# Half of an attention's transposes moved from TensorE to VectorE's 32x32 blocks and a trip to DRAM

## The chip, the cores and the metric

One core of a Trainium2 chip runs the whole kernel. The metric is the device time of one execution in microseconds; the median of three runs before the change is 898.99 us (898.84 to 899.18).

## The reference, cut to what matters

The kernel is one decoder layer on 16 sequences of 256 tokens, width 256, in float32: a self-attention on fixed keys and values with squared ReLU, a cross-attention, and a feed-forward layer with routed low-rank adapters, each followed by a layer norm. The change is in the cross-attention, which has 16 heads of 16 channels:

```python
logits = einsum('bhqd,bhkd->bhqk', Q, K) * scale
D = clip(frac[:, None, :] - frac[:, :, None], -0.2, 0.2)
attn = gamma * logits + delta * (ap * max(D, 0) + an * min(D, 0))
probs = softmax(attn, axis=-1)
out = einsum('bhqk,bhkd->bhqd', probs, V)
```

`ap` and `an` are one number for each head. The logits come with queries on the partitions, so that the maximum over keys is a reduction along a row. The product with V needs the probabilities the other way round, with keys on the partitions. So each 256x256 block of each head has to be transposed.

## The kernel before, in words

The program's order on each engine is the order in which the code issues instructions (a manual schedule). Each engine takes its own instructions in that order and waits at the first whose inputs or buffers are not ready. SyncE (SP) issues nearly all DMAs and is such a queue too.

The first 252 us are the self-attention. Then come 64 *groups*, four for each sequence (a *batch* `b`; `og = n % 4` counts its groups). A group is four heads. One turn of the loop over `n`, here called a round, works on several groups at once: `now` (group n), `nxt` (n+1), `last` (n-1) and `older` (n-2).

- `logits` (L650): 16 small matmuls (two records each in the profile) of `now` into four PSUM banks, one for each head. They add to what `positive` (L640, ScalarE) has put there, the positive part of the bias.
- `negative` (L628 on GpSimd, L633 on ScalarE): the negative part of the bias of `nxt`, into the tile `neg`.
- `maxima` (L667, VectorE): eight instructions that add the bank and `neg`, write the sum over `neg` (also called `t`) and keep the row maximum `mx`. When the two of a head are done, `nxt.positive` may overwrite that head's bank.
- `subtract` (L682): row maximum off, two heads on GpSimd, two on VectorE.
- `turned` and `exps` (L692, L699): four 128x128 transposes on TensorE (PE) for a head into a PSUM tile `ps_b`, then the exponential on ScalarE on the way into the tile `pT`. A group has 16 such transposes.
- `attend` (L708): eight matmuls with the values and a column block of ones, which gives the softmax's denominator. After a batch's second and fourth group `keep` copies the accumulators (L721), and after the fourth `gather` sends them through DMAs: `sums`, and eight `v`.

The ScalarE order in a round was written by hand as a string: `s0` is `nxt.positive(0)`, `e0` is `last.turned(0)` and `last.exps(0)`, `g` a copy of the router's logits in some rounds:

```python
for act in ("e0 s0 s1 e1 s2 s3" if eager else "s0 s1 g e0 e1 s2" if ff and part == 0
            else "s0 s1 g e0 s2 e1 s3").split():
```

Heads 2 and 3 of `last` follow at the end of the round. In between, the round works on pieces of other batches: queries, keys, values and the output projection, each a PE step of four matmuls with a copy behind it. Their DMAs stand on SP in this order over a batch: og 1 `sums` and eight `v`; og 2 `rows`, eight `kM` (keys of the next batch, laid out for the row groups) and eight `invs` (the denominators' inverses, spread over partitions from DRAM); og 3 `cT` and the fractions or clipped biases of a later batch.

From n = 15 on, feed-forward work is woven in: eight rounds (`part` 0 to 7) for 512 tokens. Parts 2 and 3 (`halved`) hold the two large pieces of the inner layer, in the same four banks between `maxima` and `positive`; parts 4 to 7 hold the outer layer (`finish`). In parts 5 and 7 (`apart`) `attend` is left to the next round, which then has two. Rounds 0 to 14 are called plain rounds.

The accumulating tiles `ps_b` turn in two or three buffers, `neg` in three, `pT` in two.

Of the kernel before, what the change touches and what calls it, by code (L numbers as in the profile page):

```python
# [9 lines left out]
FP = mybir.dt.float32  # L10
AF = mybir.ActivationFunctionType
ALU = mybir.AluOpType
AX = mybir.AxisListType

P = 128
# [3 lines left out]
BIG = 3.0e38  # L19
# [3 lines left out]
def tile_decoder_layer(ctx: ExitStack, tc: tile.TileContext, a: dict, out: bass.AP):  # L23


    nc = tc.nc
    NTOK, C = a["x"].shape
    B, S = a["frac"].shape
# [29 lines left out]
    def tile_v(tag="V"):  # L58
        return psV.tile([P, 512], FP, tag=tag, name="ps_v")
# [155 lines left out]
    drams = ctx.enter_context(tc.tile_pool(name="drams", bufs=2, space=bass.MemoryType.DRAM))  # L215
# [16 lines left out]
    if True:  # L232
# [16 lines left out]
        class Block:  # L249
            def __init__(self, tb):  # L250
                self.tb = tb
# [169 lines left out]
    if True:  # L421
# [8 lines left out]
        class Batch:  # L430
# [183 lines left out]
        class Group:  # L614
            def __init__(self, batch, og):
                self.batch = batch
                self.o, self.i = divmod(og, 2)

            def head(self, g):
                return 8 * self.o + 2 * g + self.i  # L620
# [40 lines left out]
            def maxima(self):  # L661

                self.t = self.neg
                self.mx = small.tile([P, 4, 2], FP, tag="mx", name="mx")
                for g in range(4):
                    for j in range(2):
                        nc.vector.tensor_tensor_reduce(  # L667
                            out=self.t[:, g, j, :],
                            in0=banks[g][:, j * S : (j + 1) * S],
                            in1=self.neg[:, g, j, :],  # L670
                            scale=1.0,
                            scalar=-BIG,
                            op0=ALU.add,
                            op1=ALU.max,
                            accum_out=self.mx[:, g, j : j + 1],
                        )

            def subtract(self, halves):
                for g, eng in zip((0, 2), halves):
                    rows = self.t[:, g : g + 2].rearrange("p g j k -> p (g j) k")  # L680
                    top = self.mx[:, g : g + 2].rearrange("p g j -> p (g j)").unsqueeze(2)
                    eng.tensor_tensor(rows, rows, top.to_broadcast([P, 4, S]), ALU.subtract)  # L682
# [18 lines left out]
            def attend(self):  # L701

                batch = self.batch
                if self.i == 0:
                    batch.av = tile_v()
                for k in range(2):
                    for g in range(4):
                        nc.tensor.matmul(  # L708
                            batch.av[32 * g : 32 * g + 32, self.i * S : (self.i + 1) * S],
                            lhsT=batch.va[:, k, self.head(g), :],  # L710
                            rhs=self.pT[:, g, k * S : (k + 1) * S],
                            start=(k == 0),
                            stop=(k == 1),
                        )
# [7 lines left out]
                    if self.o == 1:  # L722
                        batch.gather()

        MADE = 5
# [229 lines left out]
    with tc.manual_schedule():  # L955
# [5 lines left out]
        for j in range(WARM):  # L961
# [17 lines left out]
        for tb in range(NB):  # L979
            now = rows_in[tb]  # L980
# [6 lines left out]
            if tb > 1:  # L987
                last = rows_in[tb - 2]
# [14 lines left out]
            if tb + 1 < NB:  # L1003
                nxt = rows_in[tb + 1]
# [33 lines left out]
            for m in range(8):  # L1038
                c, n2 = divmod(m, 4)
# [22 lines left out]
        pm = ctx.enter_context(tc.tile_pool(name="pm", bufs=2))  # L1062
# [4 lines left out]
        FUSED, FIRST = NB - 2, 15  # L1067
# [6 lines left out]
        for n in range(N + 2):  # L1074
            now, nxt, last, older = (
                groups[n + d] if 0 <= n + d < N else None for d in (0, 1, -1, -2)
            )
            large_piece, small_piece, more = pieces(n)
            tb, part = divmod(n - FIRST, 8)
            ff = rows_out[tb] if 0 <= tb < FUSED or (tb == FUSED and part < 2) else None  # L1080
            halved = ff and part in (2, 3)
# [7 lines left out]
            b, og = divmod(n, 4)  # L1089
# [34 lines left out]
            if n == 29:  # L1124
                by[NB] = scaling_of(rest_mv, newton(rest_mv, near_rest, 8), 8)
            if halved:
                for g in range(2):
                    last.turned(g)
                    last.exps(g)
                if part == 2:  # L1130
                    ff.route()
                now.subtract((nc.gpsimd, nc.vector))
                if part == 2:
                    ff.biased()
                if done:
                    done.ready(newton(done.mv, done.near, 4))
                ff.inner(part - 2, range(0, 3))
                if part == 2:
                    ff.turn_um()
                ff.inner(part - 2, range(3, 4))  # L1140
                ff.lora(part - 2, scalar=(0,))
                for g in range(4):
                    nxt.positive(g)
                older.attend()
            else:


                eager = n in (12, 13, 14)
                for act in ("e0 s0 s1 e1 s2 s3" if eager else "s0 s1 g e0 e1 s2" if ff and part == 0
                            else "s0 s1 g e0 s2 e1 s3").split():  # L1150
                    g = int(act[1:] or 0)
                    if act == "g":
                        if ff and part == 1 and n < N:
                            ff.keep_gates()
                    elif act[0] == "s":
                        if act == "s3" and n == N:
                            older.attend()
                        if nxt:
                            nxt.positive(g)
                    elif last:  # L1160
                        last.turned(g)
                        last.exps(g)
                if prep and prep.tb:
                    prep.rows()
# [27 lines left out]
                prep.rows()  # L1192
            if done and not halved:
                done.ready(newton(done.mv, done.near, 4))
            if ff and part >= 4:
# [139 lines left out]
```

## Time and profile before

| | us |
|---|---|
| median of three runs | 898.99 |
| profiled execution, its own time | 898.66 |
| its span, first to last instruction | 896.9 |
| self-attention, up to the first logits | 252.4 |
| plain rounds of groups 2 to 14 (263.2 to 342.4) | 79.2 |
| rounds of groups 15 to 62, with feed-forward work (342.4 to 813.0) | 470.6 |
| the rest (813.0 to 896.9) | 83.9 |

| engine | busy us | share of the span |
|---|---|---|
| PE matmuls | 885.6 | 99% |
| VectorE (DVE) | 713.0 | 79% |
| ScalarE (ACT) | 567.1 | 63% |
| GpSimd (POOL) | 398.8 | 44% |

The profile holds one execution. A group of instructions is shown as line, engine, operation, output and inputs, count, then busy us and mean ns of one, then the engine's idle time ahead of them and what ended it. A line of the timeline starts with the start and the duration in us. DMAs took 15% of the 16 DMA engines' time, 41 GB/s in the mean.

### The profile page before, as it was taken

Reading aid. Unit: us, or ns where it says so; the run is one execution under the profiler, and the core shown is the slowest. Engines: PE = TensorE matmul, PEld = TensorE weight load, DVE = VectorE, ACT = ScalarE, POOL = GpSimd, SP = SyncE. Lnnn points to the kernel's source line nnn. Section 1 sums busy time; section 2 is a strip of 40 time slices with the busy share of each in tenths; the row PEclk is TensorE's granted clock in tenths of the full one; section 3 lists DMA queues with packets and bytes.
Section 4 is the critical chain, followed back from the end, with each engine's and each line's share of the span. In section 5 each row is a group of like instructions: output and inputs, shape, how many; then the busy total and the mean of one; then the engine's idle time right before and its main releaser. Section 6 shows DMA issues by size and latency. Waiting matters only on the chain.

```text
span 896.9 us, 21381 instructions
## 1 busy us (share of the span) xinstructions
PE 885.6 (99%) x8092; PEld 550.0 (61%) x8092; DVE 713.0 (79%) x1986; ACT 567.1 (63%) x951; POOL 398.8 (44%) x385
## 2 busy tenths in 40 slices
PE   8999999999999999999999999999999999999997
PEld 4334444444466777577668757766875776586555
DVE  6879889988779899788777877877798787778344
ACT  5766777777787888376556836666684665566111
POOL 1101223422489899435534644563465456344010
PEclk9999999999999999999999999999999999999999
DMA  5501110110001222011111202011110201111001
GB/s 138 156 1 42 53 43 25 30 49 1 14 1 55 71 69 57 14 42 25 33 50 39 48 14 67 21 36 46 43 48 14 67 20 38 44 29 43 23 2 46
DMA packets 44200, 37.15 MB, mean 41 GB/s; under 512 B 14913, under 2 KB 40001, under 8 KB 44097
## 3 DMA queue, kind: packets, MB, share of 16 engines
q1 hardware_dynamic: 43520, 35.52, 14.5%
q8 instruction: 64, 1.05, 0.5%
q10 hardware_dynamic: 576, 0.26, 0.1%
q14 instruction: 40, 0.32, 0.1%
HBM read 21.07 MB, written 6.03 MB: 30 GB/s over the span
## 4 chain that ended last, share of the span: by engine, by line
PE 97%; ACT 2%; DVE 1%; issue 0%; POOL 0%; DVEq 0%; ACTq 0%; POOLq 0%
PE ps_b L692 13%; PE ps_a L339 13%; PE ps_v L358 12%; PE ps_l L887 12%; PE ps_l L650 8%; PE ps_b L920 7%; PE ps_v L708 7%; PE ps_v L920 5%; PE ps_b L601 3%; PE ps_b L497 3%; PE ps_b L471 3%; PE ps_b L519 3%; PE ps_l L900 2%; PE ps_b L814 1%; PE ps_b L458 1%; PE ps_b L799 1%
## 5 line engine op out<-in xcount | busy, mean ns | idle before, releaser
L628 POOL TENSOR_SCALAR neg<-dneg,aneg,delta 128x512 f32<-128x512 f32 x217 | 182.0, 852 | 181.7 <-PE ps_b L692 127.3
L667 DVE CUSTOM_DVE_ANT_0 neg<-ps_l,neg 128x256 f32<-128x256 f32 x512 | 181.5, 420 | 27.7 <-PE ps_l L650 24.6
L640 ACT ACTIVATE ps_l<-dpos,apos_d 128x512 f32<-128x512 f32 x256 | 172.8, 687 | 42.0 <-DVE mx L667 26.9
L699 ACT ACTIVATE pT<-ps_b 128x512 f32<-128x512 f32 x256 | 142.3, 591 | 57.4 <-PE ps_b L692 56.2
L348 DVE TENSOR_TENSOR pr<-pr 128x1024 f32<-128x1024 f32 x128 | 153.8, 1243 | 30.2 <-ACT pr L347 29.8
L347 ACT ACTIVATE pr<-ps_a 128x1024 f32<-128x1024 f32 x128 | 125.0, 1026 | 52.9 <-PE ps_a L339 52.5
L692 PE MATMUL ps_b<-ident,neg 128*128 128x128 f32 x1024 | 139.0, 277 | 2.3 <-ACT pT L699 2.3
L692 PEld LDWEIGHTS ps_b<-ident,neg 128*128 128x128 f32 x1024 | 113.6, 141 | 37.9 <-POOL neg L628 12.7
L682 POOL TENSOR_TENSOR neg<-neg,mx 128x1024 f32<-128x1024 f32 x65 | 125.3, 1929 | 18.1 <-DVE mx L667 16.9
L339 PE MATMUL ps_a<-xnT,kT 64*64 64x512 f32 x1024 | 124.6, 593 | 1.0 <-ACT xnT L324 0.4
L358 PE MATMUL ps_v<-pr,vv 64*64 64x512 f32 x1024 | 122.7, 589 | 0.0
L887 PE MATMUL ps_l<-xt,wi 128*128 128x512 f32 x248 | 111.7, 596 | 0.0
L682 DVE TENSOR_TENSOR neg<-neg,mx 128x1024 f32<-128x1024 f32 x63 | 99.0, 1572 | 0.6
L413 POOL TENSOR_TENSOR hid<-hid,bo 128x256 f32<-128x256 f32 x32 | 43.7, 1368 | 105.0 <-ACT hid L245 86.4
L358 PEld LDWEIGHTS ps_v<-pr,vv 64*64 64x64 f32 x1024 | 45.1, 133 | 64.4 <-issue 54.5
L339 PEld LDWEIGHTS ps_a<-xnT,kT 64*64 64x64 f32 x1024 | 42.0, 133 | 65.2 <-issue 52.4
L887 PEld LDWEIGHTS ps_l<-xt,wi 128*128 128x128 f32 x248 | 45.3, 190 | 49.4 <-issue 44.4
L650 PE MATMUL ps_l<-kM,qT 32*64 32x256 f32 x2048 | 74.2, 387 | 0.0
L373 POOL TENSOR_TENSOR xt<-xt,half 128x512 f32<-128x512 f32 x15 | 19.1, 1274 | 119.2 <-ACT half L372 119.2
L920 PE MATMUL ps_b<-wof,hT 128*128 128x256 f32 x304 | 68.4, 380 | 0.0
L708 PE MATMUL ps_v<-pT,vaug 128*32 128x256 f32 x1024 | 66.5, 384 | 0.0
L913 DVE TENSOR_SCALAR hT<-ps_l,wib 128x512 f32<-128x512 f32 x43 | 29.8, 745 | 44.0 <-PE ps_l L900 44.0
(131 smaller groups left out, 1075.2 us busy)
## 6 DMA issues: line engine op xcount, KB each, us to landing
cT<-in_ctxT SPq DMA_DIRECT2D x16, 256.0 KB
kM<-keys SPq DMA_DIRECT2D x128, 32.0 KB
v<-raw SPq DMA_DIRECT2D x128, 32.0 KB
invs<-rows SPq DMA_DIRECT2D x128, 32.0 KB
x<-in_x SPq DMA_DIRECT2D x7, 512.0 KB
out<-x SPq DMA_DIRECT2D x7, 512.0 KB
frow<-in_frac SPq DMA_DIRECT2D x16, 128.0 KB
wi<-in_wiT SPq DMA_DIRECT2D x1, 1024.0 KB
```

The costliest lines, as they stand in the source:

```text
L339: nc.tensor.matmul(sc[64 * k : 64 * k + 64, h, :], lhsT=kT[64 * h : 64 * h + 64, q, hf * P + 64 * k : hf * P + 64 * k + 64], rhs=self.xnT[ ...
L348: nc.vector.tensor_tensor(pr, pr, pr, ALU.mult)
L358: nc.tensor.matmul(self.acc[k][64 * h : 64 * h + 64, :], lhsT=vv[64 * k : 64 * k + 64, hf, 64 * q : 64 * q + 64], rhs=pr[64 * k : 64 * k + ...
L628: nc.gpsimd.tensor_scalar(self.neg[:, g], self.batch.dneg, aneg[:, h : h + 1], delta, ALU.mult, ALU.mult,)
L640: nc.scalar.activation(banks[g], self.batch.dpos.rearrange("p j k -> p (j k)"), AF.Copy, scale=apos_d[:, h : h + 1],)
L650: nc.tensor.matmul(banks[g][64 * h : 64 * h + 64, j * S : (j + 1) * S], lhsT=self.batch.qT[rows, self.o, j * P + 64 * h : j * P + 64 * h + ...
L667: nc.vector.tensor_tensor_reduce(out=self.t[:, g, j, :], in0=banks[g][:, j * S : (j + 1) * S], in1=self.neg[:, g, j, :], scale=1.0, scalar ...
L682: eng.tensor_tensor(rows, rows, top.to_broadcast([P, 4, S]), ALU.subtract)
L692: nc.tensor.transpose(ps[:, k * S + j * P : k * S + (j + 1) * P], self.t[:, g, j, k * P : (k + 1) * P], ident,)
L699: nc.scalar.activation(self.pT[:, g, :], self.ps[g], AF.Exp)
L887: nc.tensor.matmul(self.banks[g], lhsT=wi[:, c, f * P : (f + 1) * P], rhs=self.xT[:, c, :], start=(c == 0), stop=False,)
L920: nc.tensor.matmul(ps[:, 0:C], lhsT=self.hT[f][:, j * P : (j + 1) * P], rhs=wof[:, f, :], start=(f == 0), stop=(f == FC - 1),)
```

## The change

From group 2 on (`DIRECT = 2`, `self.direct`), heads 0 and 1 of a group go another way:

- `maxima` of these two heads writes the negated sums and keeps their minimum.
- `exp_rows` (new, four ScalarE instructions) takes the exponential in place, in rows, with the minimum as the bias and the scale -1. So there is no `subtract` on VectorE; the one for heads 2 and 3 is on GpSimd.
- `blocks` (new): one VectorE transpose of 128x1024 in blocks of 32x32, into the tile `z` (one buffer), and one DMA of 512 KB from `z` to DRAM.
- `fetch` (new): in the next round four DMAs of 128 KB, each to 32 partitions of `pT`, bring the blocks to their places. They read what the DMA of `blocks` wrote.
- `attend` reads these two heads out of `pT` in runs of 32 elements.
- Heads 2 and 3 keep their PE transposes and `exps`, which now come in the middle of the ACT string, and there are four `exp_rows` (`x0 x1`) between them and `s2`. GpSimd makes all four of `negative`.

SP's order over a batch of plain rounds is now: fetch, write (og 0); fetch, `sums`, `v`, write (og 1); fetch, `rows`, `kM`, `invs`, write (og 2); fetch, write, `cT` and others (og 3).

```diff
+                self.direct = 4 * batch.b + og >= DIRECT
...
+                    minus = self.direct and g < 2
...
-                            scale=1.0,
-                            scalar=-BIG,
+                            scale=-1.0 if minus else 1.0,
+                            scalar=BIG if minus else -BIG,
                             op0=ALU.add,
-                            op1=ALU.max,
+                            op1=ALU.min if minus else ALU.max,
...
+            def exp_rows(self, g):
+                for j in range(2):
+                    nc.scalar.activation(
+                        self.t[:, g, j, :], self.t[:, g, j, :], AF.Exp,
+                        bias=self.mx[:, g, j : j + 1], scale=-1.0,
+                    )
+
+            def blocks(self):
+                self.z = pm.tile([P, 4, 2, 4, 32], FP, tag="z", bufs=1, name="z")
+                nc.vector.transpose(
+                    self.z.rearrange("p n c h q -> p h c n q"),
+                    self.t[:, 0:2].rearrange("p g j (c n k) -> p (g j) c n k", c=2, k=32),
+                )
+                self.away = drams.tile([P, 4, 4 * P // 2], FP, tag="blocks", name="away_z")
+                nc.sync.dma_start(
+                    out=self.away, in_=self.z.rearrange("p n c h q -> p n (c h q)")
+                )
+
+            def fetch(self):
+                self.pT = pm.tile([P, 4, 2 * S], FP, tag="pT", name="pT")
+                self.ps = {}
+                self.pD = self.pT[:, 0:2].rearrange("p g (a c h q) -> p (g a) c h q", a=2, c=2, q=64)
+                for n in range(4):
+                    nc.sync.dma_start(
+                        out=self.pT[32 * n : 32 * n + 32, 0:2].rearrange("k g (a e) -> k (g a) e", a=2),
+                        in_=self.away[:, n].rearrange("(r k) e -> k r e", k=32),
+                    )
+
             def subtract(self, halves):
-                for g, eng in zip((0, 2), halves):
+                for g, eng in ((2, nc.gpsimd),) if self.direct else zip((0, 2), halves):
...
+                        rhs = self.pT[:, g, k * S : (k + 1) * S]
+                        to = batch.av[32 * g : 32 * g + 32, self.i * S : (self.i + 1) * S]
+                        if self.direct and g < 2:
+                            rhs = self.pD[:, :, k, g, :].rearrange("p r (j q) -> p j r q", j=2)
+                            to = to.rearrange("p (j r q) -> p j r q", j=2, q=32)
...
+            if last and last.direct:
+                last.fetch()
...
-                nxt.negative(4 if 1 <= n < FIRST - 1 or (ff and part < 2) else 3)
+                nxt.negative(4 if nxt.direct or 1 <= n < FIRST - 1 else 3)
...
-                for act in ("e0 s0 s1 e1 s2 s3" if eager else "s0 s1 g e0 e1 s2" if ff and part == 0
-                            else "s0 s1 g e0 s2 e1 s3").split():
+                if n >= N or not now.direct:
+                    acts = "e0 s0 s1 e1 s2 s3" if eager else "s0 s1 g e0 s2 e1 s3"
+                    if ff and part == 0:
+                        acts = "s0 s1 g e0 e1 s2"
+                else:
+                    acts = "s0 e0 s1 g e1 x0 x1 s2" + ("" if ff and part == 0 else " s3")
...
+            if now and now.direct and not halved:
+                now.blocks()
             if ff and part >= 4:
                 ff.finish(part - 4, tile_v() if apart else None)
-            if last:
+            if last and not last.direct:
                 for g in range(2, 4):
                     last.turned(g)
                     last.exps(g)
```

In the halved rounds `exp_rows` and `blocks` stand beside `subtract`, ahead of the inner layer's pieces.

More of the change, by code (lines that the diff above doesn't have):

```diff
@@ L707, in attend @@
                     for g in range(4):
+                        rhs = self.pT[:, g, k * S : (k + 1) * S]
[3 more added lines that the diff above has]
+                            to = to.rearrange("p (j r q) -> p j r q", j=2, q=32)
                         nc.tensor.matmul(
-                            batch.av[32 * g : 32 * g + 32, self.i * S : (self.i + 1) * S],
+                            to,
                             lhsT=batch.va[:, k, self.head(g), :],
-                            rhs=self.pT[:, g, k * S : (k + 1) * S],
+                            rhs=rhs,
                             start=(k == 0),
@@ L723, in keep @@
                         batch.gather()
-        MADE = 5
+        MADE, DIRECT = 5, 2
         batches = [Batch(b) for b in range(B)]
@@ L1126, in tile_decoder_layer @@
             if halved:
-                for g in range(2):
+                for g in range(2, 4) if last.direct else range(2):
                     last.turned(g)
@@ L1131, in tile_decoder_layer @@
                     ff.route()
+                if now.direct:
+                    for g in range(2):
+                        now.exp_rows(g)
                 now.subtract((nc.gpsimd, nc.vector))
+                if now.direct:
+                    now.blocks()
                 if part == 2:
@@ L1148, in tile_decoder_layer @@
                 eager = n in (12, 13, 14)
-                for act in ("e0 s0 s1 e1 s2 s3" if eager else "s0 s1 g e0 e1 s2" if ff and part == 0
-                            else "s0 s1 g e0 s2 e1 s3").split():
+                if n >= N or not now.direct:
[4 more added lines that the diff above has]
+                    acts = "s0 e0 s1 g e1 x0 x1 s2" + ("" if ff and part == 0 else " s3")
+                for act in acts.split():
                     g = int(act[1:] or 0)
@@ L1159, in tile_decoder_layer @@
                             nxt.positive(g)
+                    elif act[0] == "x":
+                        if now:
+                            now.exp_rows(g)
                     elif last:
+                        if last.direct:
+                            g += 2
                         last.turned(g)
@@ L1194, in tile_decoder_layer @@
                 done.ready(newton(done.mv, done.near, 4))
+            if now and now.direct and not halved:
+                now.blocks()
             if ff and part >= 4:
                 ff.finish(part - 4, tile_v() if apart else None)
-            if last:
+            if last and not last.direct:
                 for g in range(2, 4):
```

## The prediction

> **What bounds the kernel now.** I read the page first: busy shares, the chain that ended last, the costliest groups.
>
> ```profile
> span 896.9 us, 21381 instructions
> PE 885.6 (99%) x8092; PEld 550.0 (61%) x8092; DVE 713.0 (79%) x1986; ACT 567.1 (63%) x951; POOL 398.8 (44%) x385
> PE 97%; ACT 2%; DVE 1%; issue 0%; POOL 0%; DVEq 0%; ACTq 0%; POOLq 0%
> L692 PE MATMUL ps_b<-ident,neg 128*128 128x128 f32 x1024 | 139.0, 277 | 2.3 <-ACT pT L699 2.3
> ```
>
> TensorE is never idle and carries the chain; the transposes that the change halves are in it. Next I asked for the chain in one round of the attention without feed-forward work (a round: from one group's logits to the next one's), and for each engine's busy time in such a round and in the eight rounds of a feed-forward cycle.
>
> ```profile
> 306.19 1.05 PE ps_l L650 x32
> 307.24 1.00 PE ps_v L708 x16
> 308.24 1.02 PE ps_b L692 x8
> 309.26 1.73 PE ps_b L601 x8
> 310.99 1.03 PE ps_b L692 x8
> ```
>
> ```profile
> 306.10:311.95 5.85, 5.85 (x73) 4.19 (x72) 5.39 (x21) 5.51 (x11) 5.43 (x5) 1.00 0.16 57
> ```
>
> ```profile
> sum 79.10, PE 79.10 PEld 55.43 DVE 64.53 ACT 49.50 POOL 39.22; mean PE 9.89 PEld 6.93 DVE 8.07 ACT 6.19 POOL 4.90
> ```
>
> (The columns behind the stretch are busy us of PE, PEld, DVE, ACT and POOL.) A plain round takes 5.83 us, with DVE, ACT and POOL close behind at 5.4 to 5.5. A feed-forward cycle has room. Last, the timelines of ACT in a plain round and of SP (which issues the DMAs) in one batch of four groups:
>
> ```profile
> 302.49 1.38 ACT L640 ACTIVATE ps_l<-dpos,apos_d 128x512 f32<-128x512 f32 x2 [1.22 <-DVE mx L667]
> 303.81 0.58 ACT L699 ACTIVATE pT<-ps_b 128x512 f32<-128x512 f32 x1
> 305.38 0.69 ACT L640 ACTIVATE ps_l<-dpos,apos_d 128x512 f32<-128x512 f32 x1
> 305.99 1.08 ACT L699 ACTIVATE pT<-ps_b 128x512 f32<-128x512 f32 x2
> ```
>
> ```profile
> 286.44 0.69 SPq L561 DMA_DIRECT2D sums<-raw  x1
> 287.18 5.86 SPq L569 DMA_DIRECT2D v<-raw  x8
> 293.15 0.52 SPq L579 DMA_DIRECT2D rows<-inv  x1
> 293.78 5.62 SPq L513 DMA_DIRECT2D kM<-keys  x8
> 299.45 3.84 SPq L587 DMA_DIRECT2D invs<-rows  x8
> ```
>
> SP holds each small DMA for about half a microsecond, so a batch costs it some 17 us; today nobody waits for that.
>
> **Removed from PE.** Eight transposes a group: 1.02 us, for 62 groups 63 us, all on today's chain.
>
> **Removed and added beside it.** VectorE loses one subtract (1.57 us mean) and gains one transpose of 128x1024; no row shows one. The subtract of that size took 1.22 us alone and 2.06 us at its slowest (304.47); I take 1.3, near the undisturbed row, so VectorE gets no fuller. It waits there for the `exp_rows` (6.04 us after the round's start, below); behind it stand the next round's maxima, due at 8.65, so up to 2.6 us are free. GpSimd gets a fourth `negative` (0.85 us) in the feed-forward rounds, where it has 4.9 of 9.9 us busy: nothing, and ACT loses a 0.72 us instruction there. Minima in place of maxima are as many instructions: nothing. `attend` reads two heads in runs of 32 elements; between 0 and 0.5 us (half of its 1.00 us doubled), taken as 0. The 1 MB a group is some 3 us of DMA at 347 GB/s (below): it fits a round.
>
> **ACT's circuit.** Before, a round's last two `exps` came after the fourth `positive`. Now everything comes before it: s0 e0 s1 e1, four `exp_rows`, s2, s3 (s is `positive`, e is `exps`), and the next logits need s3. The first s starts 2.20 us after the logits start (300.29 to 302.49). A `positive` is 0.62 (four took 2.53), the last 0.69, an `exps` 0.50. An `exp_rows` (128x256, SBUF to SBUF, bias from a tile) lies between the gT copy of 128x256, 0.27 to its successor, and L245 (x from hid) with bias and scale from tiles, 12.5 us for 24 = 0.52; I take 0.40, the middle, since it has one of the two. Sum: 2.20 + 0.62 + 0.50 + 0.62 + 0.50 + 1.60 + 0.62 + 0.69 = **7.35 us**. PE would need 5.83 - 1.02 = 4.81. So a plain round gets longer by this alone (6.83 with 0.27, 7.83 with 0.52).
>
> **SP's queue.** Each group adds a write w (512 KB, SBUF to DRAM), and a fetch f of four DMAs that cannot be issued before w has landed; SP stands at that wait, and all behind it in the queue (`sums`, `v`, `rows`, `kM`, `invs`, the next w) stands too. The order in the plain rounds, by group of the batch: f, w | f, sums, v, w | f, rows, kM, invs, w | f, w. For w I take the 512 KB store issued at 616.51: transfers stop by 619.2, so 2.65 us.
>
> ```profile
> 617.50:618.30 0.80, 0.80 (x10) 0.23 (x16) 0.00 (x0) 0.00 (x0) 0.00 (x0) 1.00 0.97 347
> 618.30:619.20 0.90, 0.90 (x22) 0.17 (x10) 0.08 (x1) 0.12 (x1) 0.00 (x0) 1.00 0.74 259
> 619.20:620.00 0.80, 0.80 (x17) 0.30 (x9) 0.80 (x2) 0.77 (x2) 0.00 (x0) 1.00 0.00 0
> ```
>
> f: four issues at 0.46 (invs: 3.84 for eight) = 1.85; landed 3.6 after the first, as the 512 KB load issued at 129.93, whose traffic ends by 133.6. Bounds: 0.40 an issue (`cT`) to 0.75 (`v` at 6.08 for eight).
>
> The circuit of a plain batch, from the end of its first group's transpose: w 2.65, f 1.85, wait for the `raw` copy 0.4, sums and v 6.45 (5.8 to 6.75 in the trace), w 2.65, f 1.85, rows, kM and invs 9.8 (0.34 to 0.52, 5.6, 3.84), w of the third group 2.65, its f landing 3.6; then `attend` 1.00, one head's transposes and their release 0.7 (ACT's e0 waits for them, and all of ACT behind it), e0 s1 e1 1.62, `exp_rows` 1.6, VectorE's transpose 1.3: 38.1, about **38 us a batch**, against 24.5 now (275.81 to 300.29). Seen from the rounds: four of 7.35, plus 1.85 of wait at the fourth group, plus 6.9 in the next batch's first round, where PE stands at `attend` of the third group.
>
> From group 2 to 15 are 13 rounds, now 79.2 us (263.2 to 342.4): 13 x 7.35 + 2 x (1.85 + 6.9) = 113.1, **+34 us**.
>
> **A feed-forward cycle.** Its rounds now last 7.98, 6.73, 14.49, 14.05, 9.57, 8.13, 9.99, 8.13 us. Each becomes the longer of itself less 1.02 and the ACT circuit. The first, with two `attend`s before e0 and two copies before s3, makes 9.4; the second has the gT copy, 7.7; the two long ones 13.47 and 13.03; then 8.55, 7.35, 8.97, 7.35. In the long rounds SP's waits are covered by feed-forward matmuls. In the eighth they are not: f until 6.95, rows to invs until 16.7, so w of that group starts at 16.7 instead of 7.4, lands at 19.35, f at 22.95 after the round's start; PE is at that `attend` at 7.35 + 9.4 + 1.05 = 17.8. **5.15 us of stall** make the second round 12.9. Sum 81.0 against 79.07: +1.9. For the first cycle (78.8 now) +2.2, for four +7.3, for the last (75.2 now, few pieces left) +5.4: **+15 us**. The rounds after group 63 are a chain of feed-forward matmuls (78.5 of 83.9 us busy): 0.
>
> **Clock.** PE now gets gaps. Granted clock is 1.00 all along, and in the tail it is 1.00 from 891.5 to 893.5, with no matmul in it, and 0.51 after. Eight stalls above 5 us could each make the following `attend` and transpose (1.5 us) twice as long: 0 to 12 us, and up to 29 more if the 2.5 us gaps of the plain rounds count too (13 x 2.2: 9.6 in place of 7.35). I take 6.
>
> [...]
>
> **The sum.** The profiled execution took 898.66 us, 0.33 below the median 898.99. 898.66 + 34 + 15 + 6 = 953.7; I say **953 us**.
>
> **Rivals.**
> *PE stays the bound.* DMAs and ACT hide; 898.7 - 63 = **835 us**. For it: a 99% busy PE and two rounds of grace between a group's exp and its `attend`. Against it: 7.35 us of ACT in front of logits that PE could start after 4.81. It needs the instructions before s3 to be near 2.5 us shorter, and SP never late.
> *ACT's circuit binds, SP does not.* If w and f always land in time, the stalls go: plain 13 x 7.35 - 79.2 = +16, cycles 81.0 - 5.15 = 75.8, six of them 455 in place of 471, -16: **about 899 us**, no change; with `exp_rows` at 0.27 about 880. This is the other side's likeliest form; it decides where a plain batch costs SP less than the four rounds' 29.4 us, not the 34 that 4 x (2.65 + 1.85) + 6.45 + 9.8 make.
> *Dearer all round.* Clock halved in the plain rounds and issues at 0.6: **about 1000 us**.
>
> **How the numbers follow.** Forecast 0.73 (own range 920 to 985), dearer 0.07, ACT's circuit alone 0.12 (a third of it within 0.2%), PE bound or near it 0.08. 0.2% is about what a measurement of this kernel can tell from no change. Faster 0.16, same 0.04, slower 0.80. The range from 897 to 1000 leaves out the faster 0.16 and 0.04 above.
>
> **What would show it.** After the change: PE well under 90% busy from 263 on; ACT, SP's waits or DMA landings in the chain; PE waiting for a DMA ahead of `attend` (pT from the blocks tile), 5 to 7 us once a batch; plain rounds of 7 us or more; SP in the timeline standing between w and f; granted clock under 1.00 somewhere. I am wrong if plain rounds stay under 6 us, if `attend` never waits, or if the transpose takes over 3 us (then VectorE is the bound).

## The result, and the profile after

The changed kernel takes **1050.24 us** (median of 4 runs, 1046.81 to 1052.71) against 899.09 for the kernel before (898.84 to 899.58): 1.168 times as long, 95% interval 1.1644 to 1.1711. The prediction said 953 us and a range up to 1000. The sign was right, the size was not: +151 us in place of +54.

From the page of the changed kernel's profiled execution (span; busy time by engine; granted clock in 40 slices; the chain that ended last; three groups):

```profile
span 1048.4 us, 21128 instructions
...
PE 917.2 (87%) x7596; PEld 527.1 (50%) x7596; DVE 717.0 (68%) x1986; ACT 577.1 (55%) x1038; POOL 412.0 (39%) x422
...
PEclk9999999999988788999898899889989997998999
...
PE 58%; DMA 11%; SPq 10%; DVE 9%; ACT 7%; issue 4%; ACTq 0%; DVEq 0%
...
L691 DVE STREAM_TRANSPOSE z<-neg 128x1024 f32<-128x1024 f32 x62 | 77.0, 1241 | 138.7 <-ACT neg L683 74.9
L746 PE MATMUL ps_v<-pT,vaug 128*32 128x256 f32 x1024 | 82.3, 452 | 87.5 <-DMA pT<-away_z 72.3
...
L683 ACT ACTIVATE neg<-neg,mx 128x256 f32<-128x256 f32 x248 | 105.2, 502 | 0.0
```

TensorE carried 97% of the chain before and carries 58% now; 21% lies with transfers and with SP's queue. TensorE's 496 missing matmuls are the transposes that went. The clock row has tenths below 9 from the twelfth slice on, 288 us after the start; a mean of 0.939 over 1048.4 us means some 128 us at half clock (1048.4 x 0.061 / 0.5).

In the waits (line of the waiting instruction, what it waits for, us in all, times, longest):

```profile
SPq L706 <- DMA away_z<-z: 126.2, 50, 4.6
...
PE ps_v L746 <- DMA pT<-away_z: 72.3, 19, 6.9
...
DVE z L691 <- DMA away_z<-z: 62.8, 17, 6.0
```

SP stands 50 times between a group's write (L696) and its fetch (L706), TensorE stands 19 times at an `attend` for the fetch, and VectorE stands 17 times ahead of its block transpose, because `z` has one buffer and the write of the group before has not landed.

By stage (the plain rounds are groups 2 to 14, the feed-forward rounds 15 to 62; "halved" is the time at half clock, whole stretches, of which the last can run past the end of the span), for all kernels that follow, in us of the profiled execution:

| kernel | plain | feed-forward | tail | halved | time |
|---|---|---|---|---|---|
| before | 79.2 | 470.5 | 83.9 | 5 | 898.66 |
| changed | 123.4 | 565.0 | 96.8 | 130 | 1050.19 |
| no_trip | 94.9 | 484.7 | 88.3 | 18 | 933.99 |
| no_trip_split | 95.0 | 475.4 | 87.9 | 15 | 924.83 |
| few_issues | 104.3 | 490.6 | 96.2 | 42 | 956.63 |
| z2_few | 105.0 | 489.2 | 97.1 | 41 | 957.48 |
| z2 | 120.9 | 562.9 | 97.0 | 122 | 1046.24 |
| no_wait | 115.4 | 551.8 | 92.0 | 106 | 1025.13 |
| warm | 121.7 | 557.4 | 95.6 | 37 | 1039.92 |
| no_trip_late | 92.1 | 503.0 | 88.8 | 41 | 949.87 |
| parts26 | 79.2 | 485.7 | 85.8 | 13 | 915.67 |
| parts23 | 79.2 | 468.7 | 84.2 | 3 | 898.11 |
| parts23_split | 79.1 | 463.2 | 84.2 | 5 | 891.71 |
| parts235_split | 79.2 | 461.7 | 85.0 | 4 | 892.31 |

One feed-forward cycle (groups 31 to 38, parts 0 to 7), from the first logits of one group to those of the next. Where two of the four heads' logits start before the last `positive`, this mark is early: in no_trip the logits of parts 0, 1 and 2 stretch over 2.8, 3.2 and 3.3 us in place of 1.1, so what this table gives to part 2 is partly missing in parts 7, 0 and 1. Counted from last logit to last logit, the cycle of no_trip reads 9.72, 8.54, 14.95, 13.62, 8.69, 7.29, 9.12, 8.78; that of before stays as it is:

| kernel | 0 | 1 | 2 | 3 | 4 | 5 | 6 | 7 | sum |
|---|---|---|---|---|---|---|---|---|---|
| before | 7.98 | 6.73 | 14.49 | 14.05 | 9.57 | 8.13 | 9.99 | 8.13 | 79.1 |
| predicted | 9.4 | 12.9 | 13.47 | 13.03 | 8.55 | 7.35 | 8.97 | 7.35 | 81.0 |
| changed | 9.21 | 16.80 | 16.67 | 13.62 | 9.18 | 7.25 | 15.59 | 7.25 | 95.6 |
| no_trip | 9.38 | 8.37 | 16.68 | 13.62 | 9.17 | 7.25 | 9.16 | 7.25 | 80.9 |
| few_issues | 9.38 | 8.38 | 16.67 | 13.62 | 9.17 | 7.25 | 9.15 | 7.26 | 80.9 |
| no_trip_split | 8.64 | 8.32 | 15.78 | 13.62 | 9.17 | 7.25 | 9.15 | 7.25 | 79.2 |
| parts23 | 7.98 | 6.73 | 15.40 | 13.31 | 9.17 | 8.13 | 9.99 | 8.13 | 78.8 |
| parts23_split | 7.98 | 6.73 | 14.49 | 13.31 | 9.17 | 8.13 | 9.99 | 8.13 | 77.9 |

Against the prediction the plain rounds are 10 us dearer (123.4 against 113.1), the feed-forward rounds 79 us (+94.5 against +15), the tail 13 us; the clock's term is contained in these. So the question for the experiments was parts 1, 2 and 6 of each cycle. My theory was SP's queue: the trip (a group's write to DRAM and the fetch back) is late because SP issues 24 small DMAs a batch between writes and fetches. The rivals were the circuit of ScalarE and VectorE (late without any trip), the single `z` buffer, SP's standing at the landing of the write, and the clock.

The chain of the changed kernel around the stall of part 1 (start us, us, what):

```profile
578.24 0.56 SPq L513
...
582.65 0.60 SPq L513
583.29 0.58 SPq L587
...
586.71 0.42 SPq L587
587.23 3.75 DMA away_z<-z
...
592.95 3.76 DMA away_z<-z
...
598.16 2.96 DMA pT<-away_z
```

Eight `kM` and eight `invs` issues, 0.42 to 0.60 us each, are themselves the chain for 9 us; behind them come two writes of 3.75 us each, with a fetch issued between them, and the last fetch. So 9 us of this chain are queue and some 10.5 us are transfers behind it. Which of the two the loss hangs on, the chain alone does not say.

### The profile page after: what moved, and what is told of

Same layout as the page of the kernel before. It is cut to its first block, busy times and chain, and to the rows that moved or that the text cites. A ratio compares the mean times of both kernels' runs of the same rounds, so it can differ in the third digit from the quotient of the medians.

```text
span 1048.4 us, 21128 instructions
## 1 busy us (share of the span) xinstructions
PE 917.2 (87%) x7596; PEld 527.1 (50%) x7596; DVE 717.0 (68%) x1986; ACT 577.1 (55%) x1038; POOL 412.0 (39%) x422
## 4 chain that ended last, share of the span: by engine, by line
PE 58%; DMA 11%; SPq 10%; DVE 9%; ACT 7%; issue 4%; ACTq 0%; DVEq 0%
PE ps_a L339 11%; PE ps_v L358 10%; PE ps_l L925 9%; PE ps_b L958 6%; DMA pT<-away_z 5%; DMA away_z<-z 5%; PE ps_l L651 5%; SPq L513 4%; PE ps_v L746 4%; SPq L587 3%; PE ps_b L725 3%; ACT neg L683 3%; PE ps_b L601 3%; DVE neg L669 3%; ACT ps_l L641 2%
## 5 line engine op out<-in xcount | busy, mean ns | idle before, releaser
L715 POOL TENSOR_TENSOR neg<-neg,mx 128x1024 f32<-128x1024 f32 x65 | 127.5, 1962 | 310.2 <-DVE mx L669 220.2
L629 POOL TENSOR_SCALAR neg<-dneg,aneg,delta 128x512 f32<-128x512 f32 x254 | 194.8, 784 | 32.2 <-ACT pT L732 20.4
L691 DVE STREAM_TRANSPOSE z<-neg 128x1024 f32<-128x1024 f32 x62 | 77.0, 1241 | 138.7 <-ACT neg L683 74.9
L746 PE MATMUL ps_v<-pT,vaug 128*32 128x256 f32 x1024 | 82.3, 452 | 87.5 <-DMA pT<-away_z 72.3
L651 PE MATMUL ps_l<-kM,qT 32*64 32x256 f32 x2048 | 119.5, 395 | 28.7 <-ACT ps_l L641 28.6
L732 ACT ACTIVATE pT<-ps_b 128x512 f32<-128x512 f32 x132 | 76.3, 588 | 102.8 <-PE ps_b L725 102.7
L683 ACT ACTIVATE neg<-neg,mx 128x256 f32<-128x256 f32 x248 | 105.2, 502 | 0.0
L746 PEld LDWEIGHTS ps_v<-pT,vaug 128*32 128x32 f32 x1024 | 32.2, 123 | 133.7 <-issue 74.0
L651 PEld LDWEIGHTS ps_l<-kM,qT 32*64 32x64 f32 x2048 | 52.4, 131 | 84.7 <-ACT ps_l L641 66.3
L725 PE MATMUL ps_b<-ident,neg 128*128 128x128 f32 x528 | 81.8, 304 | 0.7 <-ACT pT L732 0.7
L725 PEld LDWEIGHTS ps_b<-ident,neg 128*128 128x128 f32 x528 | 64.8, 155 | 32.4 <-issue 25.0
L413 POOL TENSOR_TENSOR hid<-hid,bo 128x256 f32<-128x256 f32 x32 | 43.6, 1365 | 92.3 <-ACT hid L245 80.9
```

The lines of the kernel that those rows point to most:

```text
L629: nc.gpsimd.tensor_scalar(self.neg[:, g], self.batch.dneg, aneg[:, h : h + 1], delta, ALU.mult, ALU.mult,)
L651: nc.tensor.matmul(banks[g][64 * h : 64 * h + 64, j * S : (j + 1) * S], lhsT=self.batch.qT[rows, self.o, j * P + 64 * h : j * P + 64 * h + ...
L683: nc.scalar.activation(self.t[:, g, j, :], self.t[:, g, j, :], AF.Exp, bias=self.mx[:, g, j : j + 1], scale=-1.0,)
L725: nc.tensor.transpose(ps[:, k * S + j * P : k * S + (j + 1) * P], self.t[:, g, j, k * P : (k + 1) * P], ident,)
L746: nc.tensor.matmul(to, lhsT=batch.va[:, k, self.head(g), :], rhs=rhs, start=(k == 0), stop=(k == 1),)
```

## The experiments

**no_trip: the trip to DRAM taken out.** No write, no fetch; `attend` of heads 0 and 1 reads a tile of weights in place of the transposed blocks. ScalarE's and VectorE's work stays.

```diff
-                self.away = drams.tile(...); nc.sync.dma_start(out=self.away, in_=self.z...)
-                for n in range(4): nc.sync.dma_start(out=self.pT[32 * n : 32 * n + 32, 0:2]..., in_=self.away[:, n]...)
-                self.pD = self.pT[:, 0:2].rearrange(...)
+                self.pD = wi[:, 0].rearrange("p (g a c h q) -> p (g a) c h q", g=2, a=2, c=2, q=64)
```

> Leaves out the write and the fetch; attend reads the two heads from a weight tile that is always there. Rows' exp, VectorE's transpose and ScalarE's order stay. If the queue of SyncE and the DMA landings are the loss: plain rounds near 7.3, a feed-forward cycle near 76, about 899 us. If ScalarE's circuit or VectorE's transpose is the loss: over 960.

Measured: 933.99 us, between the two. So the trip costs 116 of the 151 us, and 35 are lost without it: 15.7 in the plain rounds, which the prediction had as ScalarE's circuit (+16), 14.2 in the feed-forward rounds, where it had a gain of 16, and 4.4 in the tail. In the feed-forward rounds part 2 stands out: 16.68 us against 13.47 (14.95 by the last logit). In this run TensorE waits for ScalarE's `positive` ahead of logits, which it never did before:

```profile
PE ps_l L651 <- ACT ps_l L641: 30.2, 32, 2.0
```

Of these, 13.0 us lie in the plain rounds and 15.7 in the feed-forward rounds, nearly all ahead of the logits of parts 0 to 2.

**few_issues: the small DMAs of the kernel before, fewer.** One load each in place of the eight `kM`, eight `v` and eight `invs` loads, of the same bytes but other values; the trip is whole.

```diff
-                for i in range(2):
-                    for g in range(4):
-                        rows = slice(32 * g + HD * i, 32 * g + HD * i + HD)
-                        nc.sync.dma_start(out=self.kM[rows, i], in_=keys[rows])
+                nc.sync.dma_start(out=self.kM[:, 0], in_=keys)
```

(and likewise for `v` and `inv`)

> Write and fetch stay; the eight kM, eight v and eight invs DMAs become one each with as many elements (wrong places), so SyncE issues 21 fewer in a batch, some 12 us. If SyncE's issue time is what makes write and fetch late: 905 to 930. If it is the landing of write and fetch by themselves (4 and 4.5 us): over 1000.

Measured: 956.63 us. It lies between the two numbers, but 93.6 of the 116 us that the trip cost are gone with 21 issues a batch, and parts 1 and 6 fell from 16.80 and 15.59 to 8.38 and 9.15, where they are without any trip (in two of the six cycles part 1 still takes 10.39 and 12.97). TensorE's wait for the fetch fell from 72.3 us to this:

```profile
PE ps_v L733 <- DMA pT<-away_z: 15.7, 7, 5.2
...
SPq L693 <- DMA away_z<-z: 125.8, 46, 6.3
```

The second line is the rival that the landings had become shorter: SP still stands 125.8 us at the landing of a write, against 126.2 in the changed kernel. What went is the small issues around it.

What remains over no_trip is 22.6 us. In the tail, 8 us of it, nothing else is ready, and the last groups' trip stands open on the chain of few_issues (L693 issues the fetch there):

```profile
871.18 1.17 DVE z L678
872.36 3.10 DMA away_z<-z
875.59 0.31 SPq L693
...
876.89 3.01 DMA pT<-away_z
880.04 1.93 PE ps_v L733 x16
```

From the end of the transpose to the `attend` there are 7.7 us, even with SP free.

**z2: two buffers for `z`.** Room for it comes from dividing in place (`oT` in the tile `inv`) and one buffer each for the router's `lg` and `hot`.

```diff
-                self.z = pm.tile([P, 4, 2, 4, 32], FP, tag="z", bufs=1, name="z")
+                self.z = pm.tile([P, 4, 2, 4, 32], FP, tag="z", bufs=2, name="z")
```

> The tile z gets a second buffer (room from dividing in place and from smaller router tiles). VectorE stood 63 us, 17 times, before its transpose until the write before had landed, with the next maxima behind it. If that wait is a part of the loss by itself: 1000 to 1015. If PE would wait at attend anyway for the same late fetch: 1040 to 1050.

Measured: 1046.24 us, 4 us less than the changed kernel in single runs, and only 0.6 us below the fastest of its four (1046.81), so hardly clear of its spread. VectorE's 62.8 us of waiting for the write are gone, and TensorE waits for the fetch 84.8 us in place of 72.3. The buffer that I had left out of the prediction held VectorE up, but what VectorE was held from would only have stood in SP's queue.

**z2_few: both.**

> The changed kernel with one load each in place of the eight kM, eight v and eight invs loads (values differ) and with two buffers for z. With few loads alone it took 956.6, without the trip 934.0: 22.6 us are left to the trip itself. Theory: with SP's queue short, VectorE's wait for the single z is what is left, and with two buffers the time falls to 938-946. Rival: the landings behind the last groups and in the tail (96.2 instead of 88.3 us) and the four reads' own time are what is left, and it stays at 952-957.

Measured: 957.48 us, no less than few_issues. With the queue short, `z` has no price either; what is left is, by elimination, the trip's own length.

**no_wait: SP does not stand at the landing.** The fetch reads the blocks of the group before, which landed long ago, and `attend` gets those.

```diff
-                        in_=self.away[:, n].rearrange("(r k) e -> k r e", k=32),
+                        in_=source[:, n].rearrange("(r k) e -> k r e", k=32),   # source: the away of the group before
```

> All issues and bytes stay; each fetch reads the block that the group before wrote (old data), so SyncE does not stand between a write and its fetch. SyncE stood 126 us there. If that standing is a large part: 960 to 990. If the issues alone fill the queue (few_issues gained 94 us): 1020 to 1045.

Measured: 1025.13 us, 25 less. SP's 126.2 us between write and fetch are down to 2.3, but most of the time is not saved: TensorE still waits 54.7 us for the fetch. The fetch still stands behind the small DMAs, and it now also takes longer, 4.7 to 6.7 us from its first issue to the `attend` that waits, against 4.3 to 5.4. With few_issues, where SP stands as long as before and 94 us are saved, this says that SP's standing at the landing is not by itself what costs.

**warm: the clock alone.** Six 128x512 matmuls into a free PSUM tile ahead of the `attend`s that stall (groups 4, 8 and 12, parts 1 and 6).

```diff
+            if n in (4, 8, 12) or ff and part in (1, 6):
+                warm = tile_b()
+                for _ in range(6):
+                    nc.tensor.matmul(warm, lhsT=ident, rhs=wi[:, 0, 0:512], start=True, stop=True)
```

> Six idle matmuls of 128x512 (5.3 us) go ahead of the attend that waits longest, in groups 4, 8, 12 and in parts 1 and 6, to keep the clock up. The clock was halved for 126 us after the change. If the half clock carries a good part of the loss: 1010 to 1030. If it only lengthens work that has room: 1045 to 1060.

Measured: 1039.92 us, 10.3 less (6.9 below the fastest run of the changed kernel), with 37 us at half clock in place of 130. So halved clock is worth some 7 to 10 of the 151 us in this run. The added matmuls fill stalls, but also stand in front of an `attend` that is ready, so its full worth may be more; that is not measured.

**no_trip_late: `exp_rows` behind s3.** no_trip with the order "... e1 s2 s3 x0 x1", to shorten ScalarE's circuit ahead of the logits.

> As no_trip (no write, no fetch, attend reads a weight tile), with the four exp_rows of a round behind s3 and no longer between e1 and s2. If ScalarE's order is what no_trip still loses (934 against 899): plain rounds near 5.7 and the time at 880 to 900. If VectorE's transpose, which then waits longer for its rows, or PE's own work holds it: 920 to 940.

Measured: 949.87 us, 16 more than no_trip, against both expectations. VectorE waits for `exp_rows` ahead of its transpose for 91.1 us in place of 41.9, and the next maxima stand behind that transpose on VectorE. From last logit to last logit the first plain round takes 5.74 us, ScalarE's predicted 7.35 without the four `exp_rows`; the twelve behind it take 6.79 to 8.43. So a second circuit, through VectorE's transpose, is about as long (read from this wait, not tested by itself), and the order in the change is the better one of these two.

**parts26: direct only from part 2 to part 6.** Thirty groups go the new way, the other groups the old one.

```diff
-                self.direct = 4 * batch.b + og >= DIRECT
+                self.direct = 4 * batch.b + og >= 17 and (4 * batch.b + og - 15) % 8 in (2, 3, 4, 5, 6)
```

> The new way for the groups of parts 2 to 6 (30 groups), none for parts 7, 0 and 1 and for the plain rounds. Part 6 took 15 us with the change, 9.2 to 9.6 without the trip or with few issues, since write and fetch of parts 4 and 5 stand behind kM and invs. If that stays: six times 5 to 6 us lost against 30 us won, 895 to 910. If the queue has room without parts 7, 0 and 1: 870 to 880.

Measured: 915.6 us (4 runs), ratio 1.0192 (1.0175 to 1.0208); over both ranges. Part 6 (13.25 in place of 9.99) still waits for the fetch of part 4's group, part 2 is still long, at 15.40, and part 0 grew to 9.69.

**parts23: direct only in parts 2 and 3.** The same edit with `in (2, 3)`; the trips of these 12 groups lie under the two long rounds.

> The new way only for the groups of parts 2 and 3 of a feed-forward cycle (12 groups), whose two rounds of 14 us hide write and fetch. By the theory that the new way costs nothing where its circuit is hidden: 12 x 1.02 us less, 885 to 890. If a trip costs by itself: 899 or more.

Measured: 897.73 us (10 runs) against 899.21 (13 runs of before), ratio 0.9983 (0.9973 to 0.9993): no `attend` waits for a DMA any more, and yet almost nothing is gained. Parts 3 and 4 fall by 0.74 and 0.40, part 2 grows by 0.91. Why part 2 grows shows in the timelines (start us, us) of before and of parts23, where GpSimd's `subtract` (L682, L715) meets the router's small VectorE operations:

```profile
517.90 1.89 POOL L682 TENSOR_TENSOR neg<-neg,mx 128x1024 f32<-128x1024 f32 x1 [0.37 <-DVE mx L667]
...
519.49 0.35 DVE L843 TENSOR_TENSOR hot<-lg,top 128x32 f32<-128x32 f32 x1
```

```profile
519.64 0.19 DVE L878 TENSOR_REDUCE top<-lg 128x4 f32<-128x32 f32 x1
519.65 1.89 POOL L715 TENSOR_TENSOR neg<-neg,mx 128x1024 f32<-128x1024 f32 x1 [0.99 <-DVE lg L873]
519.86 1.73 DVE L881 TENSOR_TENSOR hot<-lg,top 128x32 f32<-128x32 f32 x1
...
523.43 0.83 PE L899 MATMUL ps_b<-ident,um 128*128 128x128 f32 x4 [0.52 <-DVE um L889]
```

Before, GpSimd took heads 0 and 1, whose maxima come first, and ended at 519.79. Now it takes heads 2 and 3, starts when all eight maxima are done, and ends at 521.54; `hot` starts at 519.86 and ends at 521.59, 0.05 behind it. It takes 1.73 us for 128x32 elements, and TensorE waits for `um`. Even in before `hot` ended at 519.84, 0.05 behind GpSimd; with GpSimd idle, in the tail of before, the same operation takes 0.19. The maxima themselves, which read one of their two inputs from PSUM, run at 0.42 beside GpSimd (in before those at 303.67 and 304.01, with GpSimd's `subtract` from 303.55 to 305.45), and at 0.41 to 0.43 in all 512 of before.

**parts23_split: GpSimd's subtract in four.** The test of that reading, in the same 12 groups.

```diff
+                if self.direct:
+                    for g in (2, 3):
+                        for j in range(2):
+                            nc.gpsimd.tensor_tensor(
+                                self.t[:, g, j, :], self.t[:, g, j, :],
+                                self.mx[:, g, j : j + 1].to_broadcast([P, S]), ALU.subtract,
+                            )
+                    return
```

> Rows on the direct path only in groups of parts 2 and 3 (12 groups), and GpSimd's one subtract over heads 2 and 3 (128x1024, 1.89 us) cut into four of 128x256. Theory: part 2 costs 15.40 us instead of 14.49 because the router's small VectorE operations end only when GpSimd's running instruction ends (128x32 `hot` 1.73 us instead of 0.35); with instructions a quarter as long such an operation waits 0.5 us at most, `hot` takes under 0.9 us, part 2 comes back to 14.5-14.9, and six cycles bring 897.7 down to 891-894 us. Rival: GpSimd's subtract is simply late, since it covers the heads whose maxima come last, and what is behind it waits for its end; four instructions end no earlier, part 2 stays at 15.3 or more and the time at 897 or more.

Measured: **892.07 us** (5 runs, 891.71 to 892.23) against 899.0, ratio 0.9923 (0.9911 to 0.9935), as the theory said. Part 2 is back at 14.49. In its timeline:

```profile
515.82 2.32 POOL L715 TENSOR_TENSOR neg<-neg,mx 128x256 f32<-128x256 f32 x4
...
517.07 0.54 DVE L889 TENSOR_TENSOR hot<-lg,top 128x32 f32<-128x32 f32 x1
517.65 0.54 DVE L890 TENSOR_TENSOR hot<-hot,rev 128x32 f32<-128x32 f32 x1
```

Four instructions of 0.58 us end at about 516.40, 516.98, 517.56 and 518.14; the two VectorE operations end at 517.61 and 518.19. The gain has two parts: GpSimd's shorter hold, and its start ahead of the last maxima (515.82; the last maximum starts at 516.29). The run doesn't divide them. The two ends, each 0.05 us behind one of GpSimd's, agree with the theory. What makes these operations end with GpSimd's, and the maxima not, no run tests.

**no_trip_split: the same split in every group, without the trip.**

> Every group from 2 on direct, without the trip to DRAM (TensorE reads a tile of weights in place of the transposed blocks), and GpSimd's subtract in four instructions. Theory: part 2 falls from 16.68 to 15-15.6 and parts 1, 3 and 4 a little, 934.0 becomes 922-929 us; what then is left over the kernel before is ACT's circuit in the plain rounds (+16) and part 2. Rival: part 2 is late through ACT (four `exp_rows` ahead of heads 2 and 3), it stays at 16.4 or more, and the time at 932-936.

Measured: 924.83 us, 9.2 under no_trip, as the theory said, though part 2 came down only to 15.78 (14.05 by the last logit). Here nothing of the trip and little of the hold is left, 528 transposes remain of 1024, and the kernel is still 26 us slower than before: 15.8 of it in the plain rounds.

**parts235_split: part 5 as well.**

> The kernel before it with groups of part 5 on the direct path too (18 groups). Theory: the stalls of parts 1 and 6 come only from groups whose attend stands in those rounds (parts 7 and 4); the group of part 5 is attended in part 7, which ran at 7.25 us with its trip in the run with parts 2 to 6, so part 6 falls from 9.99 to 9.2 and nothing stalls: 5 us less than the run with parts 2 and 3 and the split, 887-890 us. Rival: the write and the four reads of that group stand in SP's queue with the eight kM and eight invs loads of part 6 and hold those up, so that part 6 or 7 grows by 1 us or more and the time is at or over that of the run before it.

Measured: 892.05 us (5 runs, 891.03 to 892.31), ratio 0.992 (0.9906 to 0.9933): no gain over parts23_split, as the rival said, but not for the rival's reason. Part 6 fell to 9.12 in five of six cycles, as the theory had it (in the last it took 10.43), and neither 6 nor 7 waited for a DMA. Part 0 grew from 8.0 or 8.1 to between 8.3 and 8.8 in the five cycles that follow. There TensorE waits six times for VectorE, which it didn't do in parts23_split:

```profile
PE ps_v L754 <- DVE x L979: 2.2, 6, 0.7
```

So about half of the 4.4 us that five part 6 rounds saved is waited for two rounds later; the last part 6 and the tail (85.0 against 84.2) take 1.2 more. VectorE is busy for 8.38 of 8.83 us in the longest of these part 0 rounds; that it is the bound there is read from this and the wait, no run tests it.

## Why the prediction was right and wrong

Where the 151.2 us went, as differences of single runs: 93.6 to the trip standing behind the small DMAs in SP's queue (changed less few_issues), 22.6 to the trip's own length (few_issues less no_trip), 9.2 to GpSimd's `subtract` in one piece, its hold on VectorE and its late start together (no_trip less no_trip_split), 25.8 to the rest (no_trip_split less before). The steps are not independent: the first holds most of the halved clock (130 us to 42). The four runs of the changed kernel spread over 6 us, so the first term is good to a few us.

- *Removed from PE, 63 us.* Right as a count: `turned` has 528 matmuls in place of 1024, and its busy time fell from 139.0 to 81.8 us, part of that at half clock. None of it reached the end of a plain round.
- *VectorE's transpose, 1.3 us.* 1.24 measured. *`exp_rows`, 0.40 in a row.* Four took 1.70, so 0.42. *Strided reads in `attend`, 0.* Right: at full clock the eight matmuls of an `attend` take 1.07 us in the changed kernel as in before.
- *ScalarE's circuit, 7.35 us.* In no_trip ten of the thirteen plain rounds take 7.25 to 7.32 us from last logit to last logit (the others 7.60 to 8.58), and its plain stage grew by 15.7 against a predicted 16. With the waits for `positive` and the 5.74 us round of no_trip_late, this step carried by its mechanism.
- *SP's queue in the plain rounds, 38 us a batch.* The rounds of groups 4 to 7 took 39.2, those of 8 to 11 40.8. What was mis-sized is the landing: the 50 writes that SP waited for took 2.6 to 4.9 us, half of them 3.5 or more, not 2.65, and the fetch 4.3 to 5.4 from its first issue to the `attend`, not 3.6. The four issues were right where nothing held them (1.73 to 1.75; one in the timeline below took 3.02). Half clock, 37 us of it in the plain rounds, is in these sums too.
- *"In the long rounds SP's waits are covered by feed-forward matmuls. In the eighth they are not."* **This is the step that failed.** A cycle has two batches, so `rows`, `kM` and `invs` are issued twice, in part 0 and in part 4, and part 4 lies behind the long rounds. I costed one stall a cycle, 5.15 us in part 1, 31 us in all. There were two: over the six cycles the trip cost 49 us in part 1 and 27 in part 6 (changed less no_trip; 8.4 and 6.4 in the cycle of the table). The stall that I did cost had the right cause and too small a size: in that cycle the write started 17.9 us after part 7's logits (predicted 16.7), landed at 21.7 (19.35), and the `attend` started at 26.2 (22.95), after 6.60 us of waiting and at half clock. The changed kernel's timeline of the stall that I left out, in part 6:

```profile
633.88 4.99 SPq L513 DMA_DIRECT2D kM<-keys  x8
...
638.91 4.14 SPq L587 DMA_DIRECT2D invs<-rows  x8
639.45 1.25 DVE L691 STREAM_TRANSPOSE z<-neg 128x1024 f32<-128x1024 f32 x1 [0.49 <-ACT neg L683]
...
643.10 1.09 PE L725 MATMUL ps_b<-ident,neg 128*128 128x128 f32 x8
643.16 3.02 SPq L706 DMA_DIRECT2D pT<-away_z  x4
...
646.28 0.38 SPq L696 DMA_DIRECT2D away_z<-z  x1
...
650.37 1.25 DVE L691 STREAM_TRANSPOSE z<-neg 128x1024 f32<-128x1024 f32 x1 [3.53 <-DMA away_z<-z]
650.40 1.75 SPq L706 DMA_DIRECT2D pT<-away_z  x4
...
651.97 1.07 PE L746 MATMUL ps_v<-pT,vaug 128*32 128x256 f32 x16 [1.51 <-DVE x L971]
...
654.89 1.94 PE L746 MATMUL ps_v<-pT,vaug 128*32 128x256 f32 x16 [1.84 <-DMA pT<-away_z]
656.75 1.97 PE L725 MATMUL ps_b<-ident,neg 128*128 128x128 f32 x8
```

Blocks ready at 640.70 are written at 646.28, because `kM`, `invs` and the fetch of the group before come first; the write lands at 650.37, the fetch at 654.89, and then `attend` and the transposes take 1.94 and 1.97 at half clock, in place of 1.07 and 1.09. For parts 2 and 3 the cover was real: parts23 never waits for a DMA.

- *Each round "becomes the longer of itself less 1.02 and the ACT circuit".* **This failed too**, for 30 us: without any trip (no_trip) the feed-forward rounds take 484.7 us, where the prediction's sum without its stalls has 455. Counted by the last logit, in the mean of six cycles, part 2 is 1.6 over it, part 7 1.4, part 1 0.8, part 3 0.6. The change moves GpSimd's `subtract` to heads 2 and 3, and I never asked when it would now run; parts23 and the splits show what that cost: in all groups the split gives back 1.0 in part 2 and 0.5 in part 0, 9 of the 30 us. TensorE's waits for `positive` ahead of the logits of parts 0 to 2 are some 15 us of no_trip's feed-forward rounds, and as much with the split, so ScalarE is late there; no run separates what makes it late, and that part of the cause stays open.
- *VectorE has 2.6 us free.* It had not: `z` has one buffer, which I did not name. z2 prices that at 4 us or less, because another wait stood behind it.
- *Tail, 0.* 12.9, of which few_issues has 12.3: the last trip has no other work over it, and part of that is halved clock.
- *Clock, 6 us.* Some 7 to 10 by warm, which leaves 37 of the 130 halved us. I counted eight stalls above 5 us; there were 23 stretches at half clock, the shortest of 3.41 us. In the 3.41 us ahead of four of them TensorE did nothing; ahead of the other 19 it worked 0.5 to 2.45 us. Other windows of that length with 1.5 to 2.45 us of work were not followed by a stretch, so no threshold comes out of this trace.

Of the rivals, ScalarE's circuit alone ("about 899") came out, in no_trip, as 934: its plain part was right, its 16 us of gain in the cycles did not exist.

## What to carry to other kernels

Before a transfer goes into a critical path, write down everything that the issuing queue does between its producer and its consumer, for every repetition in the schedule and not just the one that looks worst: here the small loads that nobody waited for, 0.48 to 0.81 us apiece, made 94 of 151 us. Take work off a saturated engine only where the replacement's latency is covered and the next engine has room: 12 groups gave 1.5 us, and 7 with GpSimd's `subtract` in four; all 62 cost 151, and six more than 12 gave nothing. When work changes hands between heads, ask when it now runs and which short instructions on the neighbouring engine it will hold.

few_issues shows what the issue time of the small loads cost here, 93.6 us; no run issued them from another engine, so whether that would have saved it is not shown.

## What was not expected of the hardware

- A VectorE operation on 128x32 elements (`hot`) took 0.19 us with GpSimd idle (tail of before) and 1.73 us beside a GpSimd subtract, ending 0.05 us after it, in all six cycles of the changed kernel (in no_trip and parts23 the eight `hot` add up to the same 10.8 us), while the maxima, which read one input from PSUM, took 0.42 us beside it in before.
- A 512 KB write landed in 2.7 us in a plain batch (issued at 315.98, the fetch behind it at 318.71) and in 3.75 to 4.1 us in the stalls shown of parts 1 and 6; over the 50 that SP waited for it was 2.6 to 4.9. Four 128 KB reads needed 4.3 to 5.4 us from the first issue to the instruction that waits for them. No run isolates what makes the difference.
- The changed kernel's stretches at half clock lasted 3.41, 6.83 or 10.24 us, but for the last, and the work in them took longer: behind the stall in part 6 `attend` took 1.94 us and the transposes 1.97, in place of 1.07 and 1.09. No idle gap of 3.41 us stood before that stretch, which begins at 653.90: TensorE idled 1.51 us, worked 1.07 and idled 0.86.
